# Low-rank attention by halves of the positions, and a gated layer whose parts run as separate jobs

## The chip, the cores and the metric

One core of one Trainium2 chip runs the whole program in one launch. The time is device microseconds for one execution; of the kernel before, the median of three runs is shown. Smaller is better. The engines are called as in the profile: PE (TensorE, matmuls), PEld (its weight loads), DVE (VectorE), ACT (ScalarE), POOL (GpSimd), SP (SyncE, which issues the DMAs).

## What is computed

x has 4 batches of 512 positions of 256 features, float32. Four layers follow each other, each of the form x = x + layer(layernorm(x)):

```python
x = x + attn_a(_layernorm(x), W_Q, W_K, W_V, W_O, b_Q, b_K, b_V, b_O)   # 16 heads of 128, causal
x = x + ffn(_layernorm(x), conv_w, Wq, Wk, Wv, Wg, router_w, Wout)      # gated layer
x = x + attn_b(_layernorm(x), Wqa, Wqb, Wkva, Wkvb, Wout)               # low rank 64, rope, causal
x = x + ffn(_layernorm(x), conv_w, Wq, Wk, Wv, Wg, router_w, Wout)      # the same gated layer
```

Both attentions mix positions within a batch. The gated layer is transposed: its sequence runs over the four batches, separately for each of the 512 positions. For batch l it mixes with the batch before it in a convolution, projects to q, k, v and a gate, weighs the values of batches 0 to l, normalises each head's result (1/sqrt of its variance) and projects back. So batch l needs batches 0 to l-1 at the same positions only, and its positions can be split freely.

## The kernel before

Everything is float32; positions come in four tiles of 128 per batch (t = 0 to 3). Each engine takes its instructions in the order in which the program issues them, and this order is written out by hand.

**Full attention** (`attention_full`, one step for each of 64 pairs of batch and head) fills the first 800 us. Into four slots of each step, `beside()` puts one step of a side job. Side jobs are generators in two lanes, taken in turn: `norms` (layer norms, whose normed and transposed x starts the next job) and `work` (gated layers, preparation of weights). Batches 0 to 2's first gated layers run here.

**Low-rank attention** (`attention_lowrank`) follows. A unit is a batch b, an octet o of eight heads, a set s of four heads of it, and a tile t; 64 units run in the order of b, o, s, t. `score` (L1000) makes four matmuls of queries by keys, each of 128 rows (four heads by 32 positions) with t*128 + 32, 64, 96 or 128 columns; DVE masks and takes the maximum (L1008), ACT the exponential (L1011), DVE the reciprocal (L1024), POOL divides (`divide`, L1027). Two units later `turn` transposes on PE (L1035), and the result is copied out of PSUM by ACT (L1044) or, for k = 1 and t > 1, by DVE (L1042). Three units later `values` multiplies by the values (L1059) for two tiles together, DVE copies (`zTb`, L1071). `output` (L1079) multiplies an octet's result by the output weights, and DVE adds it to x (L1086); each octet adds to x by itself. `project` makes an octet's queries, four times a pair of matmuls of 512 columns (L977): DVE multiplies by cosine and sine (L915, L916) and shuffles (L921), ACT copies two quarters (L917, L918), POOL adds (L922, L923). In a slot i of a unit the order is values, score, turn, divide, projection, output, side jobs:

```python
for i in range(4):
    if u > 2 and i <= units[u - 3][3] and units[u - 3][3] % 2:
        values(u - 3, i)
    if u < n:
        score(u, i)
    if 1 < u < n + 2 and i <= units[u - 2][3]:
        turn(u - 2, i)
```

`prologue` makes the first queries and keys within the last steps of full attention.

**The gated layer** (`gated`) works on a half of a batch's positions (two tiles): POOL and DVE make the convolution (L537, L543), PE projects (L559), ACT copies (L567 to L570), POOL rotates k and q (L589 to L594), DVE multiplies q by each batch's k and sums (L647, L648), DVE and POOL weigh the values (L660) and DVE adds (L674, L680), ACT squares (L685), DVE sums (L688) and takes the root of the inverse in three iterations of small operations (L694 to L703, 128x32) and multiplies (L705), PE transposes (L711) and projects back (L719), DVE adds to x (L726), SP stores. The two halves of a batch take steps in turn (`in_turn`) as one job. The second gated layer of batch b runs beside low-rank units of batch b+1; batch 3's runs alone at the end, with no attention beside it.

The normed inputs, keys and all buffers lie in fixed slots of SBUF, named by tags. Score matmuls have three PSUM banks (`ps_sc`), transposes two (`ps_tp`), projections and outputs two (`ps_mm`), values one (`ps_pz`).

## Time and profile before

| | us |
|---|---|
| median of 3 runs | 1462.08 (1458.77 to 1462.88) |
| profiled execution, its own time | 1464.73 |
| its span | 1463.0 |
| PE busy, of the span | 1331.4 (91%) |
| DVE busy | 875.0 (60%) |
| ACT busy | 601.8 (41%) |
| POOL busy | 519.1 (35%) |

The span goes from the first to the last instruction of one profiled execution. A row of the profile names a line of the kernel, an engine, an operation with the tiles that it writes and reads, and how often it ran; then the busy time in all, the mean duration of one in ns, and the idle time just before, with what ended it. In the waits, "us in total, times, longest us" follow a pair of waiting and releasing work. In the windows view each engine's busy time is given for a stretch of the span, with the number of instructions, and PEclk is the TensorE clock that was granted, as a share of full speed. Busy times of single groups of PE overlap, since matmuls are pipelined; a float32 matmul is two instructions there. The mean granted clock of the execution is 0.964.

The page's slices of 36.6 us show the course of it, tenths of busy time and of the granted clock:

```profile
PE   7989999999999999999998789988999999788852
...
DVE  3544454553665647655467655698566765867537
ACT  3433333343343343333333246455565645453420
POOL 2311112221232223312144435575353535645333
PEclk9999999999999999999999799999999999898975
```

### The profile page before, as it was taken

How to read it: one execution, taken by the hardware profiler on the slowest of the kernel's cores; microseconds unless marked ns; L12 is line 12 of the kernel's file. 1: busy time of each engine (PE TensorE's matmuls, PEld its weight loads, DVE VectorE, ACT ScalarE, POOL GpSimd, SP SyncE). 2: the span in 40 equal slices, each digit the busy share in tenths (PEclk: the TensorE clock that was granted, in tenths of full speed). 3: DMA queues.
4: the chain of work that ended last, by engine and by line, in shares of the span. 5: the costliest groups of instructions: out<-in, count | busy, mean ns of one | idle time of the engine just before them, and what ended most of it. 6: DMA issues, size and time to landing. Idle time of an engine off the chain costs nothing.

```text
span 1463.0 us, 17042 instructions
## 1 busy us (share of the span) xinstructions
PE 1331.4 (91%) x4984; PEld 768.1 (53%) x4984; DVE 875.0 (60%) x2634; ACT 601.8 (41%) x1654; POOL 519.1 (35%) x907
## 2 busy tenths in 40 slices
PE   7989999999999999999998789988999999788852
PEld 3445555555656555565554555544555555445531
DVE  3544454553665647655467655698566765867537
ACT  3433333343343343333333246455565645453420
POOL 2311112221232223312144435575353535645333
PEclk9999999999999999999999799999999999898975
DMA  3686655643554445545344200000000000000000
GB/s 112 177 252 191 183 165 183 194 144 119 173 166 147 139 121 157 175 136 169 115 141 147 65 15 1 1 1 1 1 1 1 1 11 4 1 15 1 15 0 14
DMA packets 88140, 133.80 MB, mean 91 GB/s; under 512 B 16112, under 2 KB 69872, under 8 KB 88048
## 3 DMA queue, kind: packets, MB, share of 16 engines
q1 hardware_dynamic: 88048, 132.72, 30.5%
q8 instruction: 40, 0.66, 0.2%
q14 instruction: 52, 0.43, 0.1%
HBM read 86.29 MB, written 46.40 MB: 91 GB/s over the span
## 4 chain that ended last, share of the span: by engine, by line
PE 72%; DVE 13%; POOL 5%; ACT 4%; DMA 3%; issue 2%; SPq 1%; ACTq 0%; DVEq 0%; POOLq 0%
PE ps_mm L262 14%; PE ps_pz L350 8%; PE ps_sc L288 8%; PE ps_mm L249 7%; PE ps_mm L372 7%; PE ps_mm L559 6%; PE ps_sc L1000 5%; PE ps_pz L1059 4%; PE ps_mm L1079 3%; PE ps_tp L1035 3%; PE ps_mm L719 2%; DVE ps_sc L1008 2%; DMA way<-squares 2%; PE ps_mm L977 1%; POOL probs L1027 1%
## 5 line engine op out<-in xcount | busy, mean ns | idle before, releaser
L314 POOL TENSOR_SCALAR probs<-probs,inv 128x128 f32<-128x128 f32 (+3 forms) x256 | 135.1, 546 | 549.7 <-DVE inv L311 487.5
L299 ACT ACTIVATE probs<-ps_sc,nmax 128x128 f32<-128x128 f32 (+3 forms) x256 | 135.0, 528 | 268.6 <-DVE nmax L296 268.1
L1000 PE MATMUL ps_sc<-kTb,qTb 128*128 128x160 f32 (+15 forms) x512 | 175.5, 437 | 11.7 <-POOL qTb L923 5.1
L1011 ACT ACTIVATE probs<-ps_sc,nmax 128x160 f32<-128x160 f32 (+2 forms) x192 | 104.0, 542 | 199.1 <-DVE nmax L1008 138.3
L1008 DVE CUSTOM_DVE_ANT_0 ps_sc<-ps_sc,mask_b 128x32 f32<-128x32 f32 (+15 forms) x256 | 112.9, 444 | 91.4 <-PE ps_sc L1000 70.5
L288 PE MATMUL ps_sc<-kT,qT 128*128 128x128 f32 (+3 forms) x512 | 159.3, 434 | 1.9 <-DVE kT L276 0.9
L296 DVE CUSTOM_DVE_ANT_0 ps_sc<-ps_sc,mask_a 128x128 f32<-128x128 f32 (+3 forms) x256 | 126.3, 499 | 41.9 <-PE ps_sc L288 40.7
L350 PE MATMUL ps_pz<-probsT,v 128*128 128x512 f32 (+3 forms) x512 | 151.1, 438 | 0.0
L1027 POOL TENSOR_SCALAR probs<-probs,inv 128x160 f32<-128x160 f32 (+2 forms) x192 | 107.9, 580 | 109.5 <-DVE inv L1024 78.7
L1000 PEld LDWEIGHTS ps_sc<-kTb,qTb 128*128 128x128 f32 x512 | 84.8, 199 | 105.9 <-issue 58.9
L350 PEld LDWEIGHTS ps_pz<-probsT,v 128*128 128x128 f32 x512 | 97.6, 192 | 79.2 <-issue 58.2
L363 DVE TENSOR_SCALAR zT<-ps_pz,bias 128x512 f32<-128x512 f32 x64 | 48.0, 751 | 144.7 <-PE ps_pz L350 144.7
L262 PE MATMUL ps_mm<-xT,wk 128*128 128x512 f32 x256 | 124.3, 609 | 8.7 <-DMA wk<-in_a_wk_dram 8.5
L249 PE MATMUL ps_mm<-wv,xT 128*128 128x512 f32 x256 | 121.8, 601 | 0.0
L372 PE MATMUL ps_mm<-wo,zT 128*128 128x256 f32 x512 | 121.0, 380 | 0.0
L262 PE MATMUL ps_mm<-xT,wq 128*128 128x512 f32 x256 | 120.3, 592 | 0.0
L323 DVE STREAM_TRANSPOSE squares<-probs 128x512 f32<-128x512 f32 (+3 forms) x256 | 115.1, 487 | 0.0
L1035 PE MATMUL ps_tp<-ident,probs 128*128 128x128 f32 x576 | 93.8, 286 | 19.8 <-ACT probsT L1044 10.7
L288 PEld LDWEIGHTS ps_sc<-kT,qT 128*128 128x128 f32 x512 | 86.6, 190 | 39.2 <-issue 31.0
L256 ACT COPY v<-ps_mm 128x512 f32<-128x512 f32 x64 | 37.5, 586 | 165.1 <-PE ps_mm L249 165.1
L372 PEld LDWEIGHTS ps_mm<-wo,zT 128*128 128x128 f32 x512 | 93.7, 190 | 16.2 <-issue 4.9
L559 PE MATMUL ps_mm<-w_in,cx 128*128 128x512 f32 (+1 forms) x256 | 94.5, 505 | 5.5 <-DVE cx L550 4.2
(150 smaller groups left out, 2058.4 us busy)
## 6 DMA issues: line engine op xcount, KB each, us to landing
way<-squares SPq DMA_DIRECT2D x64, 640.0 KB, 2.9
probsT<-way SPq DMA_DIRECT2D x256, 160.0 KB, 3.3
wv<-in_a_wv_dram SPq DMA_DIRECT2D x16, 512.0 KB, 5.3
wq<-in_a_wq_dram SPq DMA_DIRECT2D x32, 256.0 KB, 3.9
wk<-in_a_wk_dram SPq DMA_DIRECT2D x32, 256.0 KB, 3.9
wo<-in_a_wo_dram SPq DMA_DIRECT2D x16, 512.0 KB, 4.9
x<-in_x_dram SPq DMA_DIRECT2D x16, 128.0 KB, 3.5
out_dram<-x SPq DMA_DIRECT2D x16, 128.0 KB, 1.7
```

Source lines behind the costliest of these rows:

```text
L249: nc.tensor.matmul(pv, lhsT=xTs[b][:, c, t * P : (t + 1) * P], rhs=wv[g][:, c, :], start=(c == 0), stop=(c == DC - 1),)
L262: nc.tensor.matmul(ps, lhsT=w[u // 2][:, c, (u % 2) * DH : (u % 2 + 1) * DH], rhs=xTs[b][:, c, :], start=(c == 0), stop=(c == DC - 1),)
L288: nc.tensor.matmul(ps[:, :m], lhsT=queries[u][:, t * P : (t + 1) * P], rhs=keys[u][:, :m], start=True, stop=True,)
L296: nc.vector.tensor_tensor_reduce(ps[:, :m], ps[:, :m], mask[:, S - m :], -1.0, 3.0e38, ALU.add, ALU.min, nmax[:, t : t + 1])
L299: nc.scalar.activation(pr[:, t, :m], ps[:, :m], AF.Exp, bias=nmax[:, t : t + 1], scale=-1.0, accum_out=total[:, t : t + 1],)
L314: nc.gpsimd.tensor_scalar(pr[:, t, :m], pr[:, t, :m], inv[:, t : t + 1], 1.0, ALU.mult, ALU.mult)
L350: nc.tensor.matmul(z[:, :, k:, :], lhsT=v[:, k, j * DH : (j + 1) * DH], rhs=pT[:, :, f : f + m, :], start=(k == 0), stop=(k == NT - 1),)
L372: nc.tensor.matmul(po[:, :D], lhsT=zTs[HG * g + i][:, t].rearrange("p i b -> p (i b)"), rhs=wo[g][:, i, :], start=(i == 0), stop=(i == HG ...
L559: nc.tensor.matmul(ps[:, : hi - lo], lhsT=cx[:, c, i * P : (i + 1) * P], rhs=w_in[:, c, lo:hi], start=(c == 0), stop=(c == DC - 1),)
L1000: nc.tensor.matmul(ps, lhsT=q[:, m // 32 - 1].rearrange("p h q -> p (h q)"), rhs=kT[:, :m], start=True, stop=True,)
L1008: nc.vector.tensor_tensor_reduce(ps, ps, lw["mask"][:, S - m :], -1.0, 3.0e38, ALU.add, ALU.min, nmax[:, i : i + 1])
L1035: nc.tensor.transpose(pt.rearrange("p (h i q) -> p h i q", h=4, i=4)[:, :, i, :], lw["probs"][t][i][:, k * P : (k + 1) * P], ident,)
```

## The change

- Low-rank attention goes by group: a batch, an octet, and a half of the positions (tiles 0 and 1, or 2 and 3). A unit is now a tile of a group; the halves of the last two batches alternate: (2,0), (3,0), (2,1), (3,1). Queries are projected by halves (matmuls of 256 columns, twice as many), and so are the rotations of keys.
- `output` waits for both octets of a half and adds them up in PSUM: eight matmuls and one addition to x per tile.
- The copies of `zTb` and of the transposed probabilities are all ACT's.
- In a slot, `turn` comes ahead of `score`. Probabilities get a second set of buffers.
- A lane can hold several jobs at once: `work` takes steps of two jobs that use different buffers (`half`), at most one step of a job in a call of `beside`. Each half of a gated layer is a job by itself; in the second layer it starts from a norm of its own two tiles once its half of the low-rank attention is done. Batch 3's second half becomes two jobs of one tile each.
- The root's iterations and `half_var` move from DVE to POOL, where an iteration takes four operations instead of three.
- In full attention of batch 3, two of the slots take two side steps; in low-rank units the number of side steps depends on the tile: 3, 4, 10 and 12 a unit. The preparation of weights goes into the `norms` lane.
- The first group's queries and keys are made in steps 60 to 64 of full attention.

The diff, cut to its core:

```diff
     class Lane:
-        def __init__(self):
-            self.jobs = []
+        def __init__(self, places):
+            self.jobs, self.places, self.turn = [], places, 0
         def add(self, *jobs):
-            self.jobs.extend(jobs)
-        def step(self):
-            while self.jobs:
-                try:
-                    return next(self.jobs[0])
-                except StopIteration:
-                    self.jobs.pop(0)
-    norms, work = Lane(), Lane()
+            self.jobs.extend((job, {}) if not isinstance(job, tuple) else job for job in jobs)
+        def active(self):
+            found = []
+            for entry in self.jobs:
+                uses = entry[1].get("half")
+                if uses is None or all(uses != other[1].get("half") for other in found):
+                    found.append(entry)
+                elif uses is not None:
+                    continue
+                if len(found) == self.places:
+                    break
+            return found
+        def step(self, done):
+            jobs = [entry for entry in self.active() if id(entry) not in done]
+            if not jobs:
+                return False
+            self.turn += 1
+            entry = jobs[self.turn % len(jobs)] if len(jobs) == self.places else jobs[0]
+            done.add(id(entry))
+            try:
+                next(entry[0])
+            except StopIteration:
+                self.jobs.remove(entry)
+            return True
+    norms, work = Lane(1), Lane(2)
...
+        done = set()
         for _ in range(times):
             lanes = [norms, work] if last_lane[0] is work else [work, norms]
-            last_lane[0] = lanes[0] if lanes[0].jobs else lanes[1]
-            last_lane[0].step()
-    def norm(b, take, extra=None):
+            for lane in lanes:
+                if lane.step(done):
+                    last_lane[0] = lane
+                    break
+    def norm(b, take, extra=None, tiles=range(NT), xT=None):
...
-            beside()
+            beside(1 + (b > 2))
...
-    def gated(layer, l, xT, xT_before, half, after):
-        tiles = range(half * HT, (half + 1) * HT)
-        rows = slice(half * HT * P, (half + 1) * HT * P)
+    def gated(layer, l, xT, xT_before, tiles, half, after):
+        nt, place = len(tiles), tiles[0] // HT
+        rows = slice(tiles[0] * P, (tiles[-1] + 1) * P)
+        first = tiles[0] % HT
+        def past(m):
+            kv, r = history[layer, m, place]
+            return kv[:, first : first + nt, :], r[:, first * H : (first + nt) * H]
...
-        nc.vector.tensor_scalar(half_var, var, -0.5, None, ALU.mult)
         nc.vector.tensor_scalar(
             root.bitcast(I32), var.bitcast(I32), -0.5, float(0x5F3759DF), ALU.mult, ALU.add
         )
+        nc.gpsimd.tensor_scalar(half_var, var, -0.5, 1.0, ALU.mult, ALU.mult)
         nc.gpsimd.tensor_tensor(o, o, gate, ALU.mult)
         yield
         for _ in range(3):
-            nc.vector.tensor_tensor(square, root, root, ALU.mult)
-            nc.vector.tensor_tensor(square, square, half_var, ALU.mult)
-            nc.vector.scalar_tensor_tensor(root, square, 1.5, root, ALU.add, ALU.mult)
+            nc.gpsimd.tensor_tensor(square, root, root, ALU.mult)
+            nc.gpsimd.tensor_tensor(square, square, half_var, ALU.mult)
+            nc.gpsimd.tensor_scalar(square, square, 1.0, 1.5, ALU.mult, ALU.add)
+            nc.gpsimd.tensor_tensor(root, root, square, ALU.mult)
...
-        octets = [(b, o) for b in range(B) for o in range(OCT)]
-        units = [(b, o, s, t) for b, o in octets for s in range(2) for t in range(NT)]
-        n, per_batch = len(units), OCT * 8
+        halves = [(0, 0), (0, 1), (1, 0), (1, 1), (2, 0), (3, 0), (2, 1), (3, 1)]
+        groups = [(b, o, half) for b, half in halves for o in range(OCT)]
+        units = [(b, o, s, 2 * half + t) for b, o, half in groups for s in range(2) for t in range(2)]
+        n = len(units)
+        HS = S // 2
...
+            both = slot("wq0", "turns").rearrange("p (a i q) -> p a i q", a=2, q=32)
+            t1, t2 = both[:, 0], both[:, 1]
+            cos, sin = (lw[name][:, half * HS // 32 : (half + 1) * HS // 32] for name in ("cos", "sin"))
+            nc.vector.tensor_tensor(t1, straight, cos, ALU.mult)
+            nc.vector.tensor_tensor(t2, straight, sin, ALU.mult)
...
+            pq = [ps_mm()[:, :HS] for _ in range(2)]
+            for ps, rows in zip(pq, (lower, upper)):
                 nc.tensor.matmul(
                     ps,
-                    lhsT=lw["wq"][half, o, p].rearrange("r s k -> r (s k)"),
-                    rhs=qas[b][half, :],
+                    lhsT=lw["wq"][rows, o, p].rearrange("r s k -> r (s k)"),
+                    rhs=qas[b][rows, half * HS : (half + 1) * HS],
...
-            to = lw["probsT"][k][:, t % 2, :]
-            if k == 1 and t > 1:
-                nc.vector.tensor_copy(to, pt)
-            else:
-                nc.scalar.copy(to, pt)
+            nc.scalar.copy(lw["probsT"][k][:, t % 2, :], pt)
...
-                if t == 1:
-                    quads[b, o, s] = slot(f"zT{1 + u // NT % 3}", "zTb").rearrange(
-                        "p (t n) -> p t n", t=NT
+                g = u // 4
+                if s == 0:
+                    quads[g] = slot(f"zT{1 + g % 2}", "zTb").rearrange("p (s n) -> p s n", s=2)
+                nc.scalar.copy(quads[g][:, s, :], open_bank.pop())
+        def output(g, t):
+            po = ps_mm()
+            for o in range(OCT):
+                for i in range(4):
+                    nc.tensor.matmul(
+                        po[:, :D],
+                        lhsT=quads[g - 1 + o][:, i // 2, t % 2 * D + i % 2 * P :][:, :P],
+                        rhs=lw["wvo"][o][:, i, :],
+                        start=(o == 0 and i == 0),
+                        stop=(o == OCT - 1 and i == 3),
                     )
-                nc.vector.tensor_copy(
-                    quads[b, o, s][:, t - 1 : t + 1, :].rearrange("p b n -> p (b n)"), open_bank.pop()
-                )
-        def output(b, o, t):
-            po = ps_mm()
-            for i in range(4):
-                nc.tensor.matmul(
-                    po[:, :D],
-                    lhsT=quads[b, o, i // 2][:, t, (i % 2) * P : (i % 2 + 1) * P],
-                    rhs=lw["wvo"][o][:, i, :],
-                    start=(i == 0),
-                    stop=(i == 3),
-                )
+            b = groups[g][0]
             nc.vector.tensor_tensor(x[b][t], x[b][t], po[:, :D], ALU.add)
...
+            elif stage == -4:
+                load_queries()
             elif stage == -3:
-                load_tables()
+                load_angles()
+                compress_queries(0)
             elif stage == -2:
                 load_keys()
-                compress_queries(0)
+                project(0, 0)()
+            elif stage == -1:
+                project(0, 2)()
+            elif stage == 0:
+                project(0, 3)()
+                buffers()
+                probs_of(0, [split(f"squares{k}", k) for k in range(2)])
+                probs_of(3, [slot("probs1", "probs3")])
+        def prologue_end(i):
+            stage = i - H * B
+            if stage == -2:
+                project(0, 1)()
             elif stage == -1:
                 compress_keys(0)
...
+        for g, (b, o, half) in enumerate(groups):
+            u = 4 * g
+            if g + 1 < len(groups):
+                for p, (j, i) in enumerate(((0, 1), (1, 0), (1, 2), (2, 1))):
+                    project_at(u + j, i, g + 1, p)
+            if o == OCT - 1:
+                for t, (j, i) in enumerate(((7, 0), (7, 2)) if half else ((6, 3), (7, 2))):
+                    at(u + j, i, output, g, 2 * half + t)
+        for b in range(1, B):
+            u = 4 * groups.index((b, 0, 0))
+            for what, j in ((compress_queries, -5), (compress_keys, -3), (compress_values, -1)):
+                at(u + j, 3, what, b)
...
-        beside_at = ((0, 1, 0, 1), (1, 1, 1, 1), (1, 1, 1, 1), (1, 2, 1, 2))
+        beside_at = ((1, 0, 1, 1), (1, 1, 1, 1), (2, 3, 2, 3), (3, 3, 3, 3))
...
+                    if 2 < u < n + 3 and i <= units[u - 3][3] and units[u - 3][3] % 2:
                         values(u - 3, i)
+                    if 1 < u < n + 2 and i <= units[u - 2][3]:
+                        turn(u - 2, i)
                     if u < n:
                         score(u, i)
-                    if 1 < u < n + 2 and i <= units[u - 2][3]:
-                        turn(u - 2, i)
                     if i == 0 and 0 < u <= n:
                         divide(u - 1)
                     if later:
                         later.pop()()
-                    if octet + 1 < len(octets) and (j, i) in pair_at:
-                        later.append(project(*octets[octet + 1], pair_at[j, i]))
-                    if u < n and octet and (j, i) in output_at:
-                        output(*octets[octet - 1], output_at[j, i])
-                    if u == n + 2 and not i:
-                        output(*octets[-1], 0)
-                        output(*octets[-1], 1)
-                    if b + 1 < B and (jb, i) in compress_at:
-                        compress_at[jb, i](b + 1)
-                    beside(beside_at[j % NT][i] * (1 if b < B - 1 else 2))
-            output(*octets[-1], 2)
-            output(*octets[-1], 3)
-        return prologue, prologue_end, loop
+                    for what, args in plan[u][i]:
+                        what(*args)
+                    beside(beside_at[units[min(u, n - 1)][3]][i])
...
+    def gated_half(layer, l, half, after=None):
+        xT = gated_in[layer][l]
+        def job():
+            yield from gated(layer, l, xT, gated_in[layer].get(l - 1), HALVES[half], half, after)
+            if half:
+                yield from finished(layer, l)
+        return job(), {"half": half}
+    def then_gated(l):
         def take(xT):
-            gated_in[layer][l] = xT
-            halves = [
-                gated(layer, l, xT, gated_in[layer].get(l - 1), half, after)
-                for half in range(2)
-            ]
-            work.add(in_turn(*halves), finished(layer, l))
+            gated_in[0][l] = xT
+            work.add(*(gated_half(0, l, half) for half in range(2)))
         return take
+    def then_gated_half(l, half):
+        def take(xT):
+            gated_in[1][l] = xT
+            if (l, half) == (B - 1, 1):
+                for t in HALVES[1]:
+                    job = gated(1, l, xT, gated_in[1][l - 1], [t], t % 2, store)
+                    work.add((job, {"half": t % 2}))
+            else:
+                work.add(gated_half(1, l, half, store))
+        return norm(l, take, tiles=HALVES[half], xT=gated_in[1].get(l))
...
+        phase = u // 8 - 1
+        if u % 8 == 4 and 0 <= phase:
+            norms.add(then_gated_half(*halves[phase]))
...
+    norms.add(then_gated_half(*halves[-1]))
     while norms.jobs or work.jobs:
-        beside()
-    run(norm(B - 1, then_gated(1, B - 1, store)))
-    while work.jobs:
-        beside()
+        beside(3)
```

## The prediction

> **What bounds the kernel now.** I read the page first: PE is busy 91% of a span of 1463.0 us, DVE 60%, ACT 41%, POOL 35%. So only 132 us are not PE's, and the question is where they lie. The windows view, cut at the stages, answers it:

> ```profile
> core 0: us, PE busy (x) PEld busy (x) DVE busy (x) ACT busy (x) POOL busy (x), PEclk, DMA share, GB/s
> 880.00:1394.00 514.00, 467.56 (x2131) 267.96 (x2130) 349.39 (x1079) 267.78 (x767) 259.68 (x417) 0.97 0.01 4
> 1394.50:1463.00 68.50, 23.33 (x64) 13.95 (x64) 39.50 (x103) 12.52 (x30) 23.11 (x38) 0.65 0.02 8
> 1250.00:1300.00 50.00, 37.66 (x156) 20.64 (x155) 39.18 (x119) 23.33 (x65) 27.07 (x44) 0.86 0.00 1
> 1340.00:1370.00 30.00, 21.44 (x100) 12.82 (x99) 25.80 (x84) 12.58 (x39) 15.40 (x22) 0.83 0.00 1
> 800.00:880.00 80.00, 63.18 (x252) 39.60 (x252) 48.85 (x157) 29.62 (x84) 35.85 (x66) 0.85 0.12 37
> ```

> Up to 800 us (full attention) PE is 96 to 100% busy after the first 100 us: nothing is to be had there. Idle PE: 17 us in the change-over at 800 to 880, 46 us in low-rank attention (880 to 1394), 45 us in the tail after the last low-rank output. In 1250 to 1300 and 1340 to 1370 DVE is busy 78% and 86%, more than PE's 75% and 71%, and the granted clock falls to 0.86 and 0.83. PE's waits in the first of these stretches:

> ```profile
> PE ps_tp L1035 <- ACT probsT L1044: 4.2, 1, 4.2
> PE ps_mm L1079 <- DVE zTb L1071: 2.9, 1, 2.9
> PE ps_tp L1035 <- POOL shift L144: 2.8, 1, 2.8
> PE ps_tp L1035 <- DVE probsT L1042: 1.2, 1, 1.2
> ```

> They are copies out of PSUM (L1042, L1044, L1071) that come late behind a crowded DVE. The timeline of the tail, the whole last gated layer with no attention left beside it:

> ```profile
> 1394.53 0.42 DVE L1086 TENSOR_TENSOR x<-x,ps_mm 128x256 f32<-128x256 f32 x1 [1.31 <-PE ps_mm L1079]
> ...
> 1406.01 13.26 PE L559 MATMUL ps_mm<-w_in,cx 128*128 128x512 f32 x32 [2.88 <-DVE cx L550]
> ...
> 1428.64 0.66 DVE L647 TENSOR_TENSOR prod<-q,kv 128x256 f32<-128x256 f32 x1 [1.12 <-POOL q L594]
> ...
> 1451.49 1.28 DVE L705 TENSOR_TENSOR o<-o,root 128x512 f32<-128x512 f32 x2
> ...
> 1459.97 0.42 DVE L726 TENSOR_TENSOR x<-x,ps_mm 128x256 f32<-128x256 f32 x1 [0.44 <-PE ps_mm L719]
> ```

> From 1394.95 (last low-rank sum into x) to 1463.0 it takes 68.05 us, a chain that goes through PE, POOL and DVE in turn.

> **The tail.** The change orders low-rank work by halves of the positions, (2,0),(3,0),(2,1),(3,1) at the end, so the first half of batch 3's gated layer runs beside (2,1) and (3,1). Only two tiles are left, as two jobs of one tile. Stage by stage, before and then after:
> - Last sum to normed x transposed: 8.6 us (1394.95 to 1403.54). Half the tiles, but POOL must first finish batch 2's last gated half (its 12 small root operations), and PE its output matmuls: I keep 9.
> - To the first L559: 2.5, after 2.2. L559: 13.3 for 32 instructions, 16 are left: 6.5. Copy of gd 0.8.
> - Rotations to the first prod: 9.0. POOL runs 24 operations on 128x128 at a pitch of 0.47; a 128x4 one (L144) has 0.20 with a pitch of 0.30. At 128x64, halfway, 0.34, 24 of them 8.1, begun 2 us earlier: 6.1.
> - Eight prod and reduce pairs: 6.5 at 0.79 a pair; half-size 0.50: 4.0.
> - Weights and sums (1435.2 to 1444.6): 9.4. POOL's parts halve from 1.5 to about 0.75: 5.2.
> - Squares and var: 3.2, after 2.1.
> - Root: 3.7 on DVE. It moves to POOL, four operations an iteration for three: 24 small ones plus half_var and o times gd: 24 x 0.30 + 2.1 = 9.3.
> - L705 to the end: 11.5 (L719's 16 instructions take 5.9); with 8, 8.0.
> After: 9 + 2.2 + 6.5 + 0.8 + 6.1 + 4.0 + 5.2 + 2.1 + 9.3 + 8.0 = 53.2. **Tail: minus 15.**

> [...] The row: on DVE each root operation takes 0.18 to 0.19 us in the tail, where POOL is idle, but L701, L702, L703 average 0.226, 0.415 and 0.322 in the low-rank stage, where POOL is at work. [...] Under attention, DVE gets rid of 3 x (0.226 + 0.415 + 0.322) + 0.56 = 3.4 us a half-layer, 30 us for nine of them; POOL takes 9 x 13 x 0.3 = 35 us. POOL was 51% busy there and would be about 60%.

> **Work moved ahead of the tail.** Half a gated layer joins the low-rank stage: L559 (30.1 + 17.1)/8 = 5.9, L719 2.0, transposes 0.6, norm 0.8: plus 9.3 us of PE.

> **Projections by halves.** 64 of N=256 in place of 32 of N=512. One is now 31.2/25 = 1.25 of PE; a half should be 0.62 plus fill. No row has this shape; the bounds are 0 and 0.16 more each (four instructions at 0.04), so 0 to 10 us: I take 5. [...]

> **Moved copies and sums.** 32 zTb copies (L1071, 0.685) and 32 probsT copies (L1042, 0.687) go from DVE to ACT: DVE minus 44 us, ACT plus 37 at 0.579. Outputs add up both octets in PSUM: PE the same, DVE minus 16 x 0.41 = 6.6. With the half-layer moved in (some 25 us of DVE), DVE over the low-rank stage: 349 - 44 - 30 - 7 + 6 + 25 = 299 of 514, 58% in place of 68%. ACT: 268 + 37 + 5 + about 10 = 320, 62%. No engine passes PE.

> **Gated jobs: where and how dense.** Before, the last four half-layers ahead of the tail (batches 1 and 2) start at unit 45 and end at 63: 4 in 18 units; after, batch 2's two halves and batch 3's first, with the end of batch 1's second, spread over units 48 to 67. From unit 6 to 31 it is denser (4 where about 2.5 were), but there DVE has room. Two jobs at once each get a step in a slot, as the two halves already did in the last batch; a step that is not ready holds what is queued behind it on DVE, ACT or POOL: POOL's divide (L1027), then PE's transposes. That price was already in the trace at 1250 to 1370.

> **Transposes ahead of scores.** They need only the divide of two units ago, so PE has work while a score bank waits for its exponential; PE waits for banks (L1000 on L1011) only 4.9 us in all. Gain 0 to 5, cost 0 to 5 where a divide is late: zero.

> **Change-over.** The first group's four projections and the keys now lie in the last full-attention steps, spread wider, and batch 2's gated layer ends two steps earlier (two more slots a step in batch 3, where DVE is 56 to 64% busy). At 800 to 820 DVE is 97% and 81% busy with both, and PE waits 5.1 us for the queries (L923). Only the query weights' load moves on SP's queue, one step ahead, past one round of attention's own loads; the weights of the other two layers are prepared in the norms' lane, four slots a step instead of two, long before batch 0's gated layer wants them. The DMA engines are about half busy (0.42 to 0.68): nothing for either. I take 8 of 17 us back, between 0 and 12.

> **Idle and clock in low-rank.** Of 46 us idle I take 16 back: 12 of the 21 us lost in 1250 to 1300 and 1340 to 1370, 4 elsewhere. In nine stretches of 10 us between 800 and 870 and between 1250 and 1360 the granted clock is 0.65 to 0.89; the missing clock times PE's busy time in each adds up to 16 us. Half of it back: 8. Against it, new waits of short units (below): 5.

> **Sum.** -15 + 9.3 + 5 - 8 - 16 - 8 + 5 = -28: span 1435. The profiled execution took 1464.73, 1.7 over its span and 0.2% over the median of 1462.08; from that median, **1434**.

> **Rivals.**
> 1. **Slower: short units.** In a first half all four units of a group are short. After a unit's last score come DVE 0.43 + 0.14, ACT 0.48 + 0.20, the reciprocal 0.17 and POOL's four divides 1.94: 3.4 us for the second tile, 2.5 for the first. The next unit's PE work has to cover it: scores 1.9, transposes 1.0, values 0.9, projection 0.7, output 1.0, some 4.7 after overlap. A gated POOL operation ahead of the divide (L660 1.26, L698 1.27, or four dependent roots 1.2) eats the slack of 1.3, and because transposes stand ahead of the scores, the next scores wait too. For it: POOL's idle before the divides is put down to DVE (60 us), a chain already tight. Against: gated steps are set fewer in first halves (3 or 4 a unit against 10 to 12). It decides from (28 + 4)/32 = 1.0 us per short unit; at 1.3 it gives 1434 + 42 = **1476**.
> 2. **Given back.** The tail shortens, but low-rank idle follows gated work wherever it stands, and nothing of the 32 us returns: -15 + 9.3 + 5 = -1: **1461**. For it: both stalls in the trace lie in gated DVE bursts. Against: DVE loses 80 us of work.
> 3. **More.** Change-over 12, low-rank idle 28 and clock 12 back, projections at 0, waits 10: -15 + 9.3 - 52 + 10 = -48: **1414**. DVE's relief speaks for it; PE's 91% in low-rank is a ceiling near.

> **Numbers.** The forecast (1420 to 1447) has 0.52, the large gain 0.14, a partial gain between forecast and given back (1447 to 1457) 0.12, given back 0.05, slower 0.17. About 0.3% (4.4 us) is what a measurement of this kernel can tell from no change: faster 0.78, same 0.05, slower 0.17. The range 1408 to 1470 leaves out some 0.06 below and 0.12 above; its upper end reaches into the slower rival, its lower end to the large gain. Gains alone: 1408 to 1457.

> **What would show it.** Last low-rank sum to the end about 53 us, with the root on POOL near 9; PE idle in low-rank near 30 and its clock at 0.98 or more; DVE near 58% there; first score of the low-rank stage without a 5 us wait for its query. Wrong if PE waits at the transposes for the divide in first halves, if DVE stands at L742 for the root, or if POOL passes 70%.

## The result, and the profile after

| | before | after |
|---|---|---|
| median (4 runs each, same chip) | 1462.16 us (1458.77 to 1462.88) | 1497.14 us (1493.32 to 1501.86) |
| profiled execution, its span | 1463.0 | 1500.1 |
| PE busy, mean granted clock | 1331.4, 0.964 | 1354.8, 0.954 |
| DVE, ACT, POOL busy | 875.0, 601.8, 519.1 | 798.4, 649.9, 594.3 |
| last low-rank sum to the end | 68.1 | 51.4 |

After is slower: ratio 1.0245, 95% interval 1.0206 to 1.0285. The forecast was 28 us less; it is 35 more. (The profiled execution of after is the slowest of its four, so the two profiles differ by 37 us.) The tail did as forecast. Its root on POOL, one iteration of one of the two jobs (timeline of after: start, us, engine, line), keeps the pitch of 0.30 us an operation:

```profile
1448.36 0.42 DVE L1122 TENSOR_TENSOR x<-x,ps_mm 128x256 f32<-128x256 f32 x1 [2.00 <-PE ps_mm L1114]
...
1485.93 0.21 POOL L737 TENSOR_TENSOR square<-root 128x16 f32<-128x16 f32 x1
1486.22 0.22 POOL L738 TENSOR_TENSOR square<-square,half_var 128x16 f32<-128x16 f32 x1
1486.53 0.20 POOL L739 TENSOR_SCALAR square<-square 128x16 f32<-128x16 f32 x1
1486.82 0.22 POOL L740 TENSOR_TENSOR root<-root,square 128x16 f32<-128x16 f32 x1
```

The loss lies between 780 us and the last low-rank sum, counted here and below to the end of its output matmul on PE: 614.5 us before, 668.3 after. The windows of after, to be held against those of before:

```profile
core 0: us, PE busy (x) PEld busy (x) DVE busy (x) ACT busy (x) POOL busy (x), PEclk, DMA share, GB/s
880.00:1448.50 568.50, 500.73 (x2276) 289.32 (x2276) 305.13 (x1083) 320.86 (x904) 317.25 (x617) 0.94 0.01 4
1448.50:1500.10 51.60, 16.50 (x44) 10.08 (x44) 23.52 (x79) 7.67 (x22) 22.30 (x74) 0.67 0.03 11
1250.00:1300.00 50.00, 41.22 (x166) 24.82 (x167) 25.11 (x89) 27.64 (x80) 27.63 (x58) 0.86 0.02 6
800.00:880.00 80.00, 64.10 (x272) 43.25 (x273) 37.39 (x148) 30.39 (x98) 35.52 (x92) 0.85 0.16 51
```

No engine but PE is crowded: from 880 us on DVE is 54% busy, ACT and POOL 56%. Yet PE is idle 68 us of 568, and its clock is 0.94 (before: 46 of 514, 0.97). What it waits for, 780 us to the last sum (releaser; us in total, times, longest), in after and then in before:

```profile
PE ps_tp L187 <- ACT xn L179: 21.3, 9, 5.3
PE ps_tp L748 <- DVE o L742: 18.1, 6, 8.7
PE ps_mm L594 <- DVE turns L950: 15.4, 8, 6.3
...
PE ps_tp L1076 <- POOL probs L1068: 1.6, 2, 1.4
```

```profile
PE ps_tp L1035 <- ACT probsT L1044: 15.4, 10, 4.2
PE ps_tp L160 <- ACT xn L152: 6.6, 5, 2.6
PE ps_tp L1035 <- DVE probsT L1042: 5.5, 7, 1.2
PE ps_sc L1000 <- POOL qTb L923: 5.1, 1, 5.1
PE ps_sc L1000 <- ACT probs L1011: 4.9, 5, 2.0
```

Before, PE stands at attention's own instructions; after, at those of side jobs (L187 norm, L594, L748 and L756 gated layer). Summed over the timeline: side jobs' 13.0 before, 69.6 after; attention's 50.7 and 18.6. One such stall, in after:

```profile
978.67 0.24 POOL L737 TENSOR_TENSOR square<-root 128x32 f32<-128x32 f32 x1
978.99 0.25 POOL L738 TENSOR_TENSOR square<-square,half_var 128x32 f32<-128x32 f32 x1
...
981.07 0.69 DVE L742 TENSOR_TENSOR o<-o,root 128x512 f32<-128x512 f32 x1 [7.93 <-POOL root L740]
981.91 1.09 PE L748 MATMUL ps_tp<-ident,o 128*128 128x128 f32 x4 [8.72 <-DVE o L742]
982.40 0.63 ACT L1052 ACTIVATE probs<-ps_sc,nmax 128x448 f32<-128x448 f32 x1 [7.91 <-DVE nmax L1049]
```

From 973.59 to 981.04 POOL works through 20 root operations of two jobs in turn (all 12 of the one, 8 of the other) and two sums of queries (L956, L957); DVE stands 7.93 us at L742, so attention's maximum (L1049) and ACT's exponential behind it stand too, and PE at L748. The windows of two microseconds around it show what that does to the clock (last columns: clock, DMA):

```profile
972.00:974.00 2.00, 1.19 (x7) 0.47 (x4) 0.84 (x3) 2.00 (x7) 1.92 (x5) 1.00 0.00 0
974.00:976.00 2.00, 0.00 (x0) 0.00 (x0) 0.00 (x0) 0.49 (x2) 1.75 (x5) 0.84 0.00 0
976.00:978.00 2.00, 0.00 (x0) 0.00 (x0) 0.00 (x0) 0.00 (x0) 1.59 (x7) 0.50 0.00 0
...
982.00:984.00 2.00, 2.00 (x9) 1.98 (x10) 0.37 (x2) 1.33 (x4) 1.92 (x6) 0.50 0.00 0
984.00:986.00 2.00, 1.74 (x5) 0.32 (x4) 1.13 (x2) 0.53 (x1) 0.66 (x3) 0.60 0.00 0
986.00:988.00 2.00, 2.00 (x14) 1.61 (x12) 0.64 (x3) 1.50 (x4) 0.00 (x0) 1.00 0.03 8
```

PE stands from 973.2 to 981.9; the clock is halved some 2 us into that and is back 3.7 us after PE has gone on. In such windows I add up PE's busy time by the missing clock: from 780 us to the last sum 19.4 us in 8 episodes before, 37.6 us in 17 after. So the 53.8 us ahead of the tail are: idle PE 24.7 more (64.9 to 89.6), clock 18.2, and some 11 of work (the prediction counted 9.3 for the half gated layer and 5 for the projections).

### The profile page after: what moved, and what is told of

Same layout as the page of the kernel before. It is cut to its first block, busy times and chain, and to the rows that moved or that the text cites. A ratio compares the mean times of both kernels' runs of the same rounds, so it can differ in the third digit from the quotient of the medians.

```text
span 1500.1 us, 17660 instructions
## 1 busy us (share of the span) xinstructions
PE 1354.8 (90%) x5112; PEld 785.7 (52%) x5112; DVE 798.4 (53%) x2572; ACT 649.9 (43%) x1796; POOL 594.3 (40%) x1245
## 5 line engine op out<-in xcount | busy, mean ns | idle before, releaser
L1049 DVE CUSTOM_DVE_ANT_0 ps_sc<-ps_sc,mask_b 128x96 f32<-128x96 f32 (+15 forms) x256 | 113.6, 445 | 146.3 <-PE ps_sc L1041 141.6
L1052 ACT ACTIVATE probs<-ps_sc,nmax 128x160 f32<-128x160 f32 (+3 forms) x224 | 114.6, 512 | 159.1 <-DVE nmax L1049 106.0
L1041 PE MATMUL ps_sc<-kTb,qTb 128*128 128x32 f32 (+15 forms) x512 | 171.9, 429 | 0.8 <-ACT probs L1052 0.6
L1068 POOL TENSOR_SCALAR probs<-probs,inv 128x160 f32<-128x160 f32 (+3 forms) x224 | 117.6, 542 | 129.6 <-DVE inv L1065 110.7
L377 PE MATMUL ps_pz<-probsT,v 128*128 128x512 f32 (+3 forms) x512 | 154.7, 446 | 0.0
L323 DVE CUSTOM_DVE_ANT_0 ps_sc<-ps_sc,mask_a 128x128 f32<-128x128 f32 (+3 forms) x256 | 126.4, 500 | 49.2 <-PE ps_sc L315 48.4
L594 PE MATMUL ps_mm<-w_in,cx 128*128 128x272 f32 (+1 forms) x256 | 99.5, 519 | 25.5 <-DVE turns L950 15.4
L1081 ACT COPY probsT<-ps_tp 128x512 f32<-128x512 f32 x160 | 93.3, 585 | 63.2 <-PE ps_tp L1076 61.8
L1076 PEld LDWEIGHTS ps_tp<-ident,probs 128*128 128x128 f32 x608 | 73.3, 147 | 72.3 <-issue 34.8
L1076 PE MATMUL ps_tp<-ident,probs 128*128 128x128 f32 x608 | 102.6, 292 | 6.0 <-DVE xT L189 2.3
```

The source lines that it names most:

```text
L323: nc.vector.tensor_tensor_reduce(ps[:, :m], ps[:, :m], mask[:, S - m :], -1.0, 3.0e38, ALU.add, ALU.min, nmax[:, t : t + 1])
L377: nc.tensor.matmul(z[:, :, k:, :], lhsT=v[:, k, j * DH : (j + 1) * DH], rhs=pT[:, :, f : f + m, :], start=(k == 0), stop=(k == NT - 1),)
L1041: nc.tensor.matmul(ps, lhsT=q[:, t % 2 * 4 + i].rearrange("p h q -> p (h q)"), rhs=kT[:, :m], start=True, stop=True,)
L1068: nc.gpsimd.tensor_scalar(probs[i][:, :m], probs[i][:, :m], inv[:, i : i + 1], 1.0, ALU.mult, ALU.mult)
L1076: nc.tensor.transpose(pt.rearrange("p (h i q) -> p h i q", h=4, i=4)[:, :, i, :], lw["probs"][t][s][i][:, k * P : (k + 1) * P], ident,)
```

## The experiments

Times are medians; each ratio is to the kernel before, with its 95% interval. "Side" and "own" are PE's idle time ahead of side jobs' and of attention's instructions, 780 us to the last low-rank sum; after: 1.0245, side 69.6, own 18.6. A tail is counted here from PE's last output matmul: 68.5 before, 51.8 after. The experiments ran on several chips, each with the kernel before beside it, so sizes are read from the ratios (0.001 is 1.5 us). Among runs 1 to 8, of those on the kernel after, only run 7 has an interval clear of after's; the sizes given for the others are uncertain by some 7 us. A profile shows one execution, and run 7's is one of its faster ones (1476.13).

**1. The root on DVE again.**

```diff
-            nc.gpsimd.tensor_tensor(square, root, root, ALU.mult)
...
+            nc.vector.tensor_tensor(square, root, root, ALU.mult)
+            nc.vector.tensor_tensor(square, square, half_var, ALU.mult)
+            nc.vector.scalar_tensor_tensor(root, square, 1.5, root, ALU.add, ALU.mult)
```

> The kernel after, with only the root's iterations and half_var back on DVE (three operations an iteration, as before). Theory A, the chain: on POOL the root is a series of small dependent operations of two jobs, DVE stands at L742 for it, behind that the exponentials and PE; the waits of PE at L748 for L742 (21 us in the trace after), the clock that falls with them and the late qTb sums behind the root on POOL all go: 25 to 45 us less, 1452 to 1472; L742's wait for POOL is gone, the tail gets some 1 to 3 us longer or shorter. Theory B, the splitting itself (short units, projections by halves that hold the one turns buffer and ps_mm, norms of two tiles): the root is a small part: 5 to 18 us less, 1479 to 1492, and PE keeps waiting for xn (L187) and turns (L594) as before. Theory C (work moved ahead without idle time given back, the clock lower for its own reasons): within 5 us of after.

1493.93 us, ratio 1.0206 (1.0174 to 1.0238); side 65.4, own 19.6. L748's waits fall from 18.2 to 10.9, the tail from 51.8 to 48.4. My first theory (A, the root's chain is the loss) falls: about 6 us of 35, 3.4 of them in the tail by the profiles.

**2. Scores ahead of transposes again.**

```diff
+                    if u < n:
+                        score(u, i)
                     if 1 < u < n + 2 and i <= units[u - 2][3]:
                         turn(u - 2, i)
-                    if u < n:
-                        score(u, i)
```

> The kernel after, with scores ahead of transposes in a slot again, nothing else. Theory A says the order is a matter of chance between the two sides: within 6 us of after (1491 to 1503). Theory B' (a late divide at the transposes stops the next scores, so that DVE and ACT also run dry) says 8 to 20 us less, 1477 to 1489, and PE's waits at L748 for the late root smaller.

1507.47 us, 1.0302 (1.0264 to 1.0339): slower than after by some 8 us, if anything. The order of the change does not cost here, against theory B', and seems to help.

**3. The kernel before with the root on POOL.** Edit 1 the other way round, on before.

> The kernel before, with only the root and half_var on POOL, four operations an iteration. Theory A: DVE stands for POOL there too, in each of the half-layers beside attention, and the two halves go in turn, so 24 operations of about 0.25 to 0.3 us stand in a row with POOL's other work between them: 10 to 30 us more, 1472 to 1492, with the tail longer by about 4 to 6 us (24 x 0.3 in place of 3.7, for the two halves together) and the rest ahead of the tail. Theory B: the root does little in the old arrangement; only the tail's 4 to 6 us: 1465 to 1469. DVE's relief would win: 1455 or less.

1470.28 us, 1.0032 (1.0009 to 1.0054); the tail of the profiled runs grows by 4.2 us. That is nearly all of the 5 us in the ratio: theory A is out here too.

**4. Copies of zTb and of the transposed probabilities on DVE again.**

```diff
-            nc.scalar.copy(lw["probsT"][k][:, t % 2, :], pt)
+            to = lw["probsT"][k][:, t % 2, :]
+            if k == 1 and t > 1:
+                nc.vector.tensor_copy(to, pt)
+            else:
+                nc.scalar.copy(to, pt)
-                nc.scalar.copy(quads[g][:, s, :], open_bank.pop())
+                nc.vector.tensor_copy(quads[g][:, s, :], open_bank.pop())
```

> The kernel after, with the copies of zTb and of the transposed probabilities with k = 1 in the second halves back on DVE (64 copies, about 44 us of DVE's work). Theory A: DVE is only 54% busy there but is what stands at waits, so copies queued behind L742 come late: 3 to 12 us more, 1500 to 1509. Theory D, ACT has become too full (its exponentials wait behind copies): 5 us or more less, 1492 or below.

1502.85 us, 1.0267 (1.0238 to 1.0296); side 72.2, own 19.9. 44 us of work moved from ACT to DVE change nothing that can be measured.

**5. Side steps spaced.** One empty `yield` more ahead of L187, L594 and L748.

> The kernel after, with one empty side step more ahead of each PE step of a side job: between the normed x and its transposes (L187), between the convolution's end and the projections (L594), between the product with the root and its transposes (L748). Until the last low-rank sum PE stands 69.6 us ahead of side jobs' instructions after (L187 25.2, L594 22.7, L748 18.2, L756 3.4), 13.0 us before; ahead of attention's own it is 18.6, before 50.7. Theory D, a side job's steps come closer together than their chain takes, so PE's part is queued before its input is there and attention waits behind it: these waits fall to 45 or less, 15 to 40 us less in all, 1455 to 1480 beside a before of 1462. Theory E, the inputs are late because DVE, ACT and POOL are behind in attention's own work, and PE would wait elsewhere: within 8 us of after; the waits move to L1076 and L1041.

1497.00 us, 1.0240 (1.0215 to 1.0264); side 48.4, but own 32.0, and still 17 episodes of low clock. Of the 21.2 us that left the side jobs 13.4 came back at attention's own instructions, nearly all at the transposes (L1076 in after; 7.3 there, 20.2 here), as theory E said, and the tail grew by 4.2. An empty step moves where PE stands more than how long: the sum goes from 88.2 to 80.4, the clock loss from 37.6 to 33.6, the time not measurably.

**6. Side steps ahead of the projection in a slot.**

```diff
+                    beside(beside_at[units[min(u, n - 1)][3]][i])
                     for what, args in plan[u][i]:
                         what(*args)
-                    beside(beside_at[units[min(u, n - 1)][3]][i])
```

> The kernel after, with a slot's side steps ahead of its projection, compression or output (instead of behind it), nothing else. The gated projections L594 wait 15.4 us for DVE's turns (L949, L950), which hold both ps_mm banks after a projection of the same slot. Theory D with the banks: these waits fall to under 6, and 5 to 14 us are gained, 1483 to 1492; E, they are only the sign of a late DVE: within 5 us of after, waits at L1018 in their place.

1491.82 us, 1.0206 (1.0164 to 1.0248); L594's idle 22.7 to 9.0. As expected, though not clear of after's interval: about 6 us, with the wait for the banks that a projection of the same slot holds (L594 for L950) down from 15.4 to 0.9.

**7. Fewer side steps.**

```diff
-        beside_at = ((1, 0, 1, 1), (1, 1, 1, 1), (2, 3, 2, 3), (3, 3, 3, 3))
+        beside_at = ((1, 0, 1, 1), (1, 1, 1, 1), (1, 2, 1, 2), (2, 2, 2, 2))
```

> The kernel after with fewer side steps in second halves: 3, 4, 6 and 8 a unit instead of 3, 4, 10 and 12; the last jobs end later, so some of batch 2's second half and batch 3's first half is left for the tail. Theory D: PE's idle time ahead of side jobs' instructions falls from 69.6 by 15 to 30, the tail (last low-rank sum to the end, 51.3) grows by 8 to 25; in all between 15 us less and 5 more. Theory E: the idle time stays (within 8), and the tail's growth is lost on top: 5 to 25 us more.

1480.98 us, 1.0144 (1.0092 to 1.0195): some 15 us less, the largest single step. Side 48.3, own 25.8, clock loss 21.2 us instead of 37.6. Its windows, low-rank and tail:

```profile
780.00:1416.92 636.92, 562.11 (x2576) 330.48 (x2576) 349.10 (x1259) 352.30 (x1015) 359.32 (x721) 0.96 0.04 12
1416.92:1474.40 57.48, 19.68 (x57) 11.79 (x56) 26.82 (x90) 8.79 (x24) 29.17 (x93) 0.64 0.04 14
```

PE is busy 562.1 us ahead of the tail (after: 578.8) although only 3 us of its work went to the tail: the rest goes with the clock.

**8. As many side steps, spread evenly** over the units: `((2, 1, 2, 2), (2, 2, 2, 2), (2, 1, 2, 2), (2, 2, 2, 2))`.

> The kernel after with the side steps spread evenly over units: 7, 8, 7 and 8 a unit instead of 3, 4, 10 and 12. A slot takes about 1.4 us in tile 0, 2.2 in tiles 1 and 2, 3.7 in tile 3. Theory D: in first halves a job's steps then follow each other within 1.4 to 2.2 us instead of about 3.6, in second halves not more slowly than before, since a job never took more than one step a slot: PE's idle time ahead of side jobs' instructions grows, 5 to 20 us more. Rival: it is the number of steps in one slot that counts (three in a row), and taking two instead gives 5 to 20 us back.

1490.32 us, 1.0195 (1.0169 to 1.0221): some 7 us less, in the rival's range. By place the profiles show both: in batch 0's first half, where side steps went from 3 and 4 to 7 and 8 a unit, PE's idle time ahead of side jobs rises from 8.5 to 20.2 as theory D said; in its second half, where they went from 10 and 12 to 7 and 8, it falls from 16.3 to 8.8.

**9, 10. Both kernels without the second gated layer.** It is left out, x is stored as it is after the third layer:

```diff
-            norms.add(norm(b - 1, then_gated(1, b - 1, store)))
+            for t in range(NT):
+                store(b - 1, t)
```

> The kernel before without the second gated layer (left out in all four batches; the third layer's result is stored as it is): low-rank attention by octets alone, with only batch 3's first gated layer beside it at the start. PE loses three layers of about 18.6 us (L559 47.2/4 = 11.8, L719, transposes, norm) ahead of the last low-rank sum and some of the idle time: the last sum near 1320 instead of 1394.5, and the end a few us after it. It is the base for the next run.

> The kernel after without the second gated layer in the same way: low-rank attention by groups alone. Theory B, splitting itself costs (twice the projections, short units, chains of a unit that nothing covers): 20 us or more above the run of before without the layer, from batch 1's first score to the last sum alone 12 or more. Theory D, the loss comes with side jobs' steps, which are queued ahead of their inputs: from batch 1's first score to the last sum within 6 us of the other (projections cost 7.4 us of PE more, outputs and scores 8 less), in all at most 15 above it, which come from the change-over and batch 3's first gated layer.

1311.42 us (1307.34 to 1314.29) without it before, 1344.10 (1339.29 to 1347.06) without it after: 32.7 us more, with no second gated layer and no tail worth the name. Neither theory fits: the total is B's, but from batch 1's first score to the last sum it is 341.2 and 348.0, 6.7 us more, near D's 6 and far from B's 12. The windows of both, first before and then after:

```profile
780.00:1304.62 524.62, 488.11 (x2239) 279.35 (x2238) 322.34 (x1013) 268.98 (x775) 250.63 (x404) 0.97 0.05 14
```

```profile
780.00:1341.13 561.13, 507.38 (x2374) 296.35 (x2372) 270.21 (x1041) 314.22 (x912) 279.07 (x541) 0.94 0.05 15
```

Of 36.5 us, PE's idle time makes 17.3 (36.5 to 53.8) and its clock 13.0 (12.4 in 4 episodes to 25.4 in 10). By place: the first score 6.3 us later (819.2, 825.4), batches 0 and 1 with batch 3's first gated layer 16.0 (267.6, 283.6), batches 2 and 3 with nothing beside them 14.3 (217.8, 232.1). The idle time that is added stands ahead of side jobs' instructions (8.1 before, 28.9 after), not of attention's (27.5, 23.5). The long stalls of the split version all lie ahead of 1010 us, where the norms and batch 3's first gated layer still run; the timeline has two of 5 us and more:

```profile
832.48 1.18 PE L187 MATMUL ps_tp<-ident,xn 128*128 128x128 f32 x4 [5.04 <-ACT xn L179]
980.24 1.09 PE L748 MATMUL ps_tp<-ident,o 128*128 128x128 f32 x4 [8.63 <-DVE o L742]
```

Batches 2 and 3 show splitting by itself. The first line is run 9, both batches; the second and third are run 10, first the two first halves, then the two second halves. Below stand PE's waits in the first halves:

```profile
1086.80:1304.63 217.83, 214.34 (x1054) 124.35 (x1052) 119.81 (x397) 119.34 (x354) 95.92 (x158) 1.00 0.02 8
1109.00:1207.00 98.00, 90.43 (x480) 57.92 (x478) 44.02 (x221) 58.73 (x202) 50.02 (x100) 0.97 0.02 6
1207.00:1341.14 134.14, 133.84 (x643) 72.90 (x642) 56.56 (x198) 87.01 (x221) 56.11 (x92) 1.00 0.02 6
```

```profile
PE ps_mm L1018 <- DVE turns L950: 2.9, 4, 0.8
PE ps_mm L978 <- DVE turns L950: 1.7, 1, 1.7
PE ps_tp L1076 <- POOL probs L1068: 1.5, 2, 1.0
```

PE stalls only in the first halves, where all units are short: 7.6 us idle, most of it at projections that wait for DVE to read their banks (L1018 and L978 for L950, 4.6 us), and 3.4 us of clock. Second halves have 0.3 us. The rest of the 14.3, some 6.5 us, is PE's busy time at full clock.

**11. Before, without the layer, with each projection in two parts** of 256 columns, its rotation too.

```diff
+            for cols in parts:
+                for ps, half in zip(pq, (lower, upper)):
+                    nc.tensor.matmul(
+                        ps[:, cols],
+                        lhsT=lw["wq"][half, o, p].rearrange("r s k -> r (s k)"),
+                        rhs=qas[b][half, cols],
...
```

> The kernel before without the second gated layer, with each projection made as two of 256 columns, and its rotation in two parts (twice the instructions on PE, DVE, ACT and POOL; buffers as before, so that no part waits for the other). Theory B2, the halved shape by itself: PE has 256 instructions of 0.18 us of its own time in place of 128 of 0.28, 10 us more, and the small operations of DVE, ACT and POOL stay covered: 1317 to 1325 beside 1311.4 with whole ones. Theory B3, order and chains of short units alone cost, not the shape: within 4 us.

1316.99 us beside 1311.42: 5.6 us for the shape by itself by medians, 7.9 between the profiled spans, 10 by the ratios to before (0.9009, 0.8938), since the two ran on different chips.

**12. After, without the layer, two buffers for turned queries, batches in plain order.**

```diff
-            both = slot("wq0", "turns").rearrange(...)
+            used[0] += 1
+            both = slot(("wq0", "wk1")[used[0] % 2], "turns").rearrange(...)
-        halves = [(0, 0), (0, 1), (1, 0), (1, 1), (2, 0), (3, 0), (2, 1), (3, 1)]
+        halves = [(b, half) for b in range(B) for half in range(2)]
```

> The kernel after without the second gated layer, with the batches in plain order (no gated layer follows them here) and two buffers for the turned queries instead of one, taken by turns (the second is free once the compressed queries need only one). Without the layer, after took 1344.1 and before 1311.4; DVE waited there 24 us for POOL's qTb sums that still read the one buffer (L949), PE 13 us for L950 in all. Theory B1, the one buffer is a main part of what splitting costs: 10 to 20 us less, 1324 to 1334, L949's wait for POOL under 5. Theory B2, it costs a few us at most, since PE has other work most of the time; the rest are twice the instructions, the clock and the change-over: 1338 to 1346.

1323.97 us (1319.84 to 1329.75), 20 less than run 10 by medians, 16 by the ratios (0.9050, 0.9160). Idle 53.8 to 42.0, clock loss 25.4 to 16.4. Batches 0 and 1, whose order is the same in both, gain 10.7; batches 2 and 3 gain 11.0, and have 1.0 us of idle time left and a clock of 1.00.

**13. One wait for the buffer taken away otherwise,** in after's own order and without the layer: DVE writes the cosine products to their places (one operation more), two sine buffers take turns.

```diff
-            nc.vector.tensor_tensor(t1, straight, cos, ALU.mult)
+            nc.vector.tensor_tensor(second[lower], straight[lower], cos[lower], ALU.mult)
+            nc.vector.tensor_tensor(first[upper], straight[upper], cos[upper], ALU.mult)
```

> The kernel after without the second gated layer, in its own order of batches, with the cosine products written by DVE straight to their places in qTb and kTb (two operations of 64 rows instead of one of 128), so that only the sine products need a buffer, of which two fit where one pair stood. It takes the one buffer out of the run with two buffers and leaves its plain order of batches out. 1344.1 us with one buffer, 1324.0 with two and plain order. Theory B1, the buffer: 1322 to 1333. Theory order: the buffer is little of it, and 1336 to 1346 remain (the compression of batch 3 lies in short units then).

1342.44 us (1341.23 to 1344.11), 1.7 less than run 10 by medians, 2 more by the ratios (0.9175, 0.9160): no change that can be measured. DVE's wait for POOL's sums at the products (32 us in run 10: 23.8 for qTb, 8.5 for kTb) is gone, and yet batches 0 and 1 gain 1.1 and batches 2 and 3 gain 3.5. Either the buffer is not what counts in run 12, or the 35 us that DVE is busier here (305.4, 270.2) give it back.

**14. Runs 1, 6 and 7 together.**

> The kernel after with three edits together: thinner side steps (3, 4, 6 and 8 a unit), the root on DVE, a slot's side steps ahead of its projection. Alone they gave about 15, 6 and 6 us against after. Theory D adds them up: 1462 to 1475, PE's idle time ahead of side jobs' instructions below 40 (69.6 after). If they took away the same waits, it stays at 1476 to 1485.

1467.68 us, 1.0019 (1.0004 to 1.0034): 0.2% over before, 33 us under after, with attention split as in after. Side 36.2, own 20.7, clock loss 25.4; the last output matmul at 1407.9, the tail 54.8. It is as the prediction's second rival (given back) had it: the tail 13.8 us shorter than before, the part ahead of it 13.4 longer.

**15. Run 14 with thinner steps still** (3, 4, 4 and 6 a unit).

> The same as the run before it with thinner side steps still: 3, 4, 4 and 6 a unit. Theory D: idle time ahead of side jobs' instructions falls further, to 20 to 35, and the last low-rank sum comes 8 to 20 us earlier; the jobs left over then lengthen the tail by 12 to 30 us: between 8 us less and 15 more than the run before it.

1492.45 us, 1.0173 (1.0141 to 1.0205). 25 us more than run 14, outside what was expected. The last sum comes 12.8 us earlier (1395.0), but the tail takes 97.0 instead of 54.8: what is not done beside attention is paid in full, and more.

**16. Run 14 with the edit of run 13.**

> The kernel after with thinner side steps, the root on DVE, side steps ahead of the projection (1467.7 us together, 1.0019 of before) and the cosine products in place with two buffers for the sine products. Theory B1 with D: another 6 to 15 us less, 1452 to 1462, below before. If the waits for the buffer were covered by those for side jobs: 1463 to 1469.

1474.77 us, 1.0071 (1.0056 to 1.0085): 7 us worse than run 14 where 6 to 15 less were expected, DVE busier by 31 (405.7, 374.7).

**17, 18. Parts of the change on the kernel before:** transposes ahead of scores; then with it all copies on ACT.

> The kernel before with transposes ahead of scores in a slot, nothing else. In the kernel after the reverse edit cost 9 us. If the order helps by itself (PE has transposes to do while a score bank waits for its exponential): 1448 to 1458 beside 1462. If it helped only with short units: within 4 us of before.

> The kernel before with transposes ahead of scores and the copies of zTb and of the transposed probabilities all on ACT. DVE, 68% busy in low-rank attention, loses 64 copies of 0.69 us, 44 us. If DVE's crowd was behind before's waits at L1035 and L1079: 6 to 20 us less than before. If ACT's exponentials then come late: as much or more than the run before it.

Transposes ahead of scores alone: 1464.63 us, 1.0012 (1.0000 to 1.0024), nothing. With the copies on ACT: 1460.19 us, 0.9974 (0.9964 to 0.9985); DVE's busy time falls from 408.7 to 371.8 us, attention's own waits only from 47.9 to 42.5. The 6 to 20 us expected of it did not come; it is the fastest kernel of all here, but by less than the 0.3% named in the prediction.

## Why the prediction was wrong

**Where it held.** The tail: forecast minus 15, measured minus 16.7, with the root at 8.4 us from the first `half_var` to the second L742 (forecast 9.3) and its pitch at POOL's own row (0.30). The moved half-layer (9.3) and the projections were not measured apart; PE's work ahead of the tail grew by 11 in all. Halved projections: forecast 5 (0 to 10), measured 5.6 to 10 (run 11). In the low-rank windows, at clocks of 0.97 and 0.94, PE's busy time is 0.312 us an instruction before (L977, 100 in 31.15) and 0.194 after (L1018, 212 in 41.23), 0.039 over half: close to the prediction's upper bound (0.04). Shares of DVE, ACT and POOL: forecast 58, 62 and 60%, measured 54, 56 and 56%. No run shows the plus 6 on DVE and plus 5 on ACT that stand in these sums for halved rotations: in after DVE's three operations take 2.62 us for two halves (0.421, 0.414, 0.475 each) instead of 2.12, ACT's two copies 1.45 (0.368, 0.355 each) instead of 1.16, which is 16 and 9 us for 32 projections.

**Where it failed.** The step that failed is the one on idle time and clock ahead of the tail. The terms "change-over minus 8", "idle minus 16", "clock minus 8" and "new waits of short units plus 5" gave minus 27; what side steps cost that are not ready was put at nothing new ("That price was already in the trace at 1250 to 1370"). Ahead of the tail, less the two costs that were counted, stand 53.8 - 9.3 - 5 = 39.5 us more. That is the whole error. That side steps carry most of it is shown by run 14: three edits, to their number, their place in a slot and their root, leave attention split and take 33 of the 35 us back; run 7, their number alone, takes 15. Term by term:
- *Change-over.* First low-rank score 827.1 instead of 821.1. The first group's queries, batch 2's gated layer and the norms run there with more side steps to a slot than before, and PE meets them before they are ready (in after 2.5 us at L748, 2.8 at L756, and 5.0 at L187 just behind the first score). No run undoes this part alone.
- *Idle.* Attention's own waits fell by 32 us, twice what I took. But I counted them as gone, and PE's queue then stands at side jobs' instructions, 57 us more. The prediction's sentence "a step that is not ready holds what is queued behind it" was right; its price, "already in the trace", was not. "From unit 6 to 31 it is denser, but there DVE has room" took a share of busy time for an answer to a question about chains: a step whose input came late waited all the same (DVE stood 7.93 us at L742 in a stage where it was 54% busy). Fewer steps gave 15 us (run 7), even ones 7 (run 8), steps ahead of the projection about 6 (run 6); empty steps between them gave nothing (run 5), which speaks for how many stand in a slot rather than for the distance within a job; it is argued, not shown.
- *Clock.* I had it follow fewer stalls; it followed more: 18 us lost, not 8 gained.
- *Short units.* Rival 1 gave the right side, with a wrong mechanism and 21 us too little: PE waits for the divide only 1.6 us. Without the second gated layer 33 us of loss remain (runs 9 and 10), but most of them lie where norms and batch 3's first gated layer still run; with nothing beside, splitting costs 14.3 us over batches 2 and 3: 4.4 of idle time and 3.4 of clock, in the short units and at the banks of their projections, and 6.5 of busy time.
- *The root on POOL.* I priced POOL's time, not that DVE stands at L742 while attention's own work is queued behind it, though the prediction names just that as what would show it wrong. It costs about 6 us of the 35 (run 1), 5 on the kernel before (run 3); but 3.4 and 4.2 of these lie in the tail, where it was priced.
- *Transposes ahead of scores.* I took zero; it seems to be worth some 8 us in the change's own arrangement (run 2) and is worth nothing in the one before (run 17).

**Open.** Which part of run 12's gain is the second buffer and which the order is not settled, as run 13 shows; in the first two batches, where the order is the same, the second buffer goes with 10.7 us. The second buffer as such was not tried in the change's own order of batches. The two side steps in a slot of batch 3's full attention and the norms of two tiles (PE waits 25.2 us at L187, the longest of all) were not tried alone. How run 14's 33 us divide among its three edits is shown only for run 7's; alone they add up to 27. Nor is it shown what the 6.5 us of PE's busy time are that batches 2 and 3 have more.

## What to carry to other kernels

Finer parts that shorten a tail are paid for in the steady stage (here the tail gained 16.7 us, and batches 2 and 3 with nothing beside them lost 14.3): count there what splitting doubles, which buffer or bank each half now has to wait for, and how many steps of side work each short slot gets. Work moved ahead of the tail has to be set so thinly that no engine meets it before its inputs are there, and yet be done before the tail begins (here run 14 lies between after and run 15, which were both slower); busy shares do not show that (after's were 54 to 56% on DVE, ACT and POOL), chains do. Price every PE stall twice: once as idle time, once as clock (from 780 us to the last sum 64.9 and 19.4 us before, 89.6 and 37.6 after).

## What was not expected of the hardware

The granted clock fell before PE had stood for long. At the 8.7 us stall above it was halved 2.2 us after PE had stopped (973.19, 975.35) and full again 3.7 us after PE had gone on (981.91, 985.59). And after a gap of 1.97 us (1051.05 to 1053.01, waiting for xn) the trace of after shows a fall too:

```profile
1050.00:1052.00 2.00, 1.04 (x4) 0.32 (x2) 1.97 (x8) 1.02 (x5) 1.63 (x5) 1.00 0.00 0
1052.00:1054.00 2.00, 0.88 (x4) 0.40 (x4) 1.27 (x6) 2.00 (x7) 1.44 (x2) 0.96 0.00 0
1054.00:1056.00 2.00, 1.94 (x6) 1.25 (x6) 0.51 (x1) 0.94 (x3) 0.00 (x0) 0.50 0.00 0
1056.00:1058.00 2.00, 2.00 (x10) 1.03 (x10) 1.00 (x4) 0.63 (x3) 0.46 (x1) 0.68 0.00 0
```
